# First layer: queries times summed keys and values, head by head on two halves of the TensorE array

## The chip, the cores and the metric

The kernel runs on one core of a Trainium2 chip. A core has five engines with queues of their own: TensorE (PE: products and transposes), VectorE (DVE), ScalarE (ACT), GpSimd (POOL) and SyncE (SP, which here issues DMAs). PE's loading of a stationary operand has a row of its own in the profile, PEld. Matrix results go to PSUM, which has eight banks of 128 partitions x 512 f32. The metric is the device time of one execution in microseconds. Before the change it is 1399.87 us, the median of three runs (1397.45 to 1400.35).

## The reference

Eight sequences x[b] of 512 positions with 512 features go through two attention layers. The first, which the change touches, has eight heads of 64 features and normalises queries and keys apart from each other:

```python
xn = _ln(x, ln_w, ln_b)
q = xn @ Wq + bq
k = xn @ Wk + bk + (1.0 - src_mask) * -1000000.0
q = softmax(q.reshape(b, t, h, dh), axis=-1)      # over a head's 64 features
k = softmax(k.reshape(b, t, h, dh), axis=1)       # over the 512 positions
v = ((xn @ Wv + bv) * src_mask).reshape(b, t, h, dh)
att = einsum('bnhd,bnhl->bhdl', k, v)             # one 64 x 64 matrix per head
y = einsum('bnhd,bhdl->bnhl', q, att).reshape(b, t, d)
hh = _ln(y, ln2_w, ln2_b) * (1.0 + scale) + shift # scale, shift: from the condition
return x + silu(hh) @ W_out + b_out
```

The second layer is attention with 16 heads of 32 features and a softmax over 512 positions. The change leaves it alone.

## The kernel before

**Tiling.** P = 128; a sequence (a block, b = 0 to 7) has four chunks c of 128 positions and its features four groups i of 128, which are two heads each, u = 0 and 1. Weights and activations of the projections are split into a high and a low part (type f32r) and multiplied in three combinations, 12 products of 128x128x512 for each output tile (`project`, L852). The products of this change are plain f32.

**First layer, per block.** `l0_k` (L910) makes the keys' exponentials. `values` (L863) makes the values, `l0_kn` (L928) transposes the keys' exponentials. `l0_att` (L941) sums keys times values over the positions: 32 products of 128x64x64, two heads in two halves of the array's columns. It scales the result into `ab` (buffer `bWk`, one copy): for each feature group i a 128x130 matrix with the two heads' 64x64 blocks on its diagonal, zeros elsewhere, and two columns of ones, one per head. `l0_q` (L967) makes the queries' exponentials. `l0_y` (L982) transposes them (`qT`, buffer `yT`: features on partitions) and multiplies each chunk of `qT` by `ab`. The ones' columns give each head's sum of exponentials, so VectorE takes the reciprocal of these (`rd`) and multiplies (`y`, buffer `xc`). Then come `normalize` (L772), `hidden` (L874) and `output` (L896). The loop over b puts `l0_y` of the block before between the key products of the next: `run(mix(l0_y(b - 1), first, 4, 6))` (L1341) takes four steps of the one, then six of the other, a step ending at each `yield`.

**The order of the work.** Nothing is issued as it is written. Every call is recorded as an operation with an estimated duration (`_takes`: an f32 product takes 1.668 ns per moving column and at least 62). A planner (`Order.pack`, L368) then simulates the engines. Each takes the ready operation with the lowest key, which is the order of writing in the first of 12 rounds and afterwards the latest start by the round before; the round with the shortest planned end is issued, each engine's instructions in the order of planned starts. `order.together(takes)` (L228) makes one operation of several PE calls, with the given duration. Where PE passes between such a group and single calls the planner adds ENTER = 95 or LEAVE = 150 ns (L180, L452). All PSUM tiles of names `mm`, `S`, `ST`, `a` share the eight banks, given out in the order of writing, except that a later tile may take one if two or more are free. In the profile every instruction has L483, the line that issues the recorded calls; operations are told apart by their tiles, and PSUM tiles all read `mm`.

Of the kernel before, what the change touches and what calls it, by code (L numbers as in the profile page):

```python
# [14 lines left out]
F32 = mybir.dt.float32  # L15
F32R = mybir.dt.float32r
AF = mybir.ActivationFunctionType
ALU = mybir.AluOpType
# [3 lines left out]
P = 128  # L22
# [2 lines left out]
EPS = 1e-5  # L25
MASK = 1.0e6
MM = 216
TR = 107

COLS = {"ln_w": 4, "ln_b": 4, "ln2_w": 4, "ln2_b": 4, "b_emb": 8, "mask": 32}  # L30
# [156 lines left out]
class Room:  # L187
# [19 lines left out]
    def next(self):  # L207
        if self.free and self.head in self.queue:
            return self.queue.pop(self.head)
        if self.loose and len(self.free) > 1 and self.queue:  # L210
            return self.queue.pop(min(self.queue, key=lambda i: self.queue[i].key))
# [317 lines left out]
def kernel(ctx: ExitStack, tc: tile.TileContext, x, cond, mask0, mask1, w0, w1, out):  # L529
    real, order = tc.nc, Order(tc)  # L530
    nc = order
# [6 lines left out]
    sm = order.pool(ctx.enter_context(tc.tile_pool(name="sm", bufs=2)), each=2)  # L538
# [7 lines left out]
    def big(tag, name, dtype=F32, shape=(P, 512)):  # L546
        t = sb.tile(list(shape), dtype, name=name, tag=tag, bufs=BUFS[tag])
        if tag == "stk":
            nc.gpsimd.memset(t[:, :, 0:1].bitcast(F32), 0.0)
        return t  # L550

    def bank(tag, name, parts=P):
        tag = {"S": "mm", "ST": "mm", "a": "mm"}.get(tag, tag)
        return ps.tile([parts, 512], F32, name=name, tag=tag, bufs=BANKS[tag])
# [4 lines left out]
    def chunk(i):  # L559
        return slice(i * P, (i + 1) * P)  # L560
# [174 lines left out]
    def prep_emb(l):  # L735
        ssb = []
        for h in range(2):
            ep = mm_bank(f"ep{l}{h}")
            for t in range(2):
                raw = W[l]["we"][2 * h + t]  # L740
                for cg in range(4):
# [3 lines left out]
                    )  # L745
                yield 4 * MM
            ev = big("y", f"ev{l}{h}")
            nc.vector.tensor_copy(ev, ep)
            sp = mm_bank(f"sp{l}{h}")
            for j in range(ND):  # L750
                nc.tensor.matmul(sp[:, 8 * j : 8 * j + 8], ev[:, chunk(j)], sel8, start=True, stop=True)
                yield 2 * MM
            t = const.tile([P, ND, 8], F32, name=f"emb{l}{h}")
# [18 lines left out]
    def normalize(srcs, tag, dve=False):  # L772
        s, n = tag[0], len(srcs)
        mv = sm.tile([P, NC, 2], F32, name=f"mv{tag}", tag="mv" + s)
        for c in range(n):
            st = sm.tile([P, 6], F32, name=f"st{tag}{c}", tag="st" + s)
            nc.vector.bn_stats(st, srcs[c])
            nc.vector.bn_aggr(mv[:, c, :], st)
        ve = sm.tile([P, NC], F32, name=f"ve{tag}", tag="ve" + s)
        nc.gpsimd.tensor_scalar(ve[:, :n], mv[:, :n, 1], 1.0, EPS, ALU.mult, ALU.add)  # L780
        rstd = sm.tile([P, NC], F32, name=f"rs{tag}", tag="rs" + s)
        nc.gpsimd.tensor_tensor(rstd[:, :n], ve[:, :n], mhalf[:, :n], ALU.pow)
        if not dve and "L1" in tag:
            nm = sm.tile([P, NC], F32, name=f"nm{tag}", tag="nm" + s)
            nc.gpsimd.tensor_tensor(nm[:, :n], mv[:, :n, 0], rstd[:, :n], ALU.mult)
            nc.gpsimd.tensor_scalar(nm[:, :n], nm[:, :n], -1.0, 0.0, ALU.mult, ALU.add)
            for c in range(n):
                nc.scalar.activation(srcs[c], srcs[c], AF.Identity, bias=nm[:, c : c + 1], scale=rstd[:, c : c + 1])
            return
        if not dve:  # L790
            nm = sm.tile([P, NC], F32, name=f"nm{tag}", tag="nm" + s)
            nc.gpsimd.tensor_scalar(nm[:, :n], mv[:, :n, 0], -1.0, 0.0, ALU.mult, ALU.add)
        for c in range(n):
            if dve:
                nc.vector.tensor_scalar(
                    srcs[c], srcs[c], mv[:, c, 0:1], rstd[:, c : c + 1], ALU.subtract, ALU.mult
                )
                continue
            nc.gpsimd.tensor_scalar(
                srcs[c], srcs[c], nm[:, c : c + 1], rstd[:, c : c + 1], ALU.add, ALU.mult  # L800
            )
# [34 lines left out]
    def transpose_x(l, b, tag="mm"):  # L836
# [3 lines left out]
        for j in range(ND):  # L840
            tp = bank(tag, f"xp{l}{b}{j}")
            for c in range(NC):
                nc.tensor.transpose(tp[:, chunk(c)], xs[c][:, chunk(j)], ident)
                yield TR
            h, o = alloc(j)
# [6 lines left out]
    def project(pt, left, right, lsl, rsl):  # L852
        n = 3 * ND
        i = 0
        for a, r in ((0, 0), (0, 1), (1, 0)):
            for j in range(ND):
# [3 lines left out]
                i += 1  # L860
                yield MM

# [11 lines left out]
    def hidden(l, b, tag="mm"):  # L874
# [4 lines left out]
        for j in range(ND):  # L879
            tp = bank(tag, f"hp{l}{b}{j}")  # L880
            for c in range(NC):
                nc.tensor.transpose(tp[:, chunk(c)], ys[c][:, chunk(j)], ident)
                yield TR
            h, o = alloc(j)
# [43 lines left out]
    def l0_kn(b):  # L928
        ke = st.pop(("ke", b))
        kn = []  # L930
        for c in range(NC):
            tp = bank("S", f"kt{b}{c}")
            for i in range(4):
                nc.tensor.transpose(tp[:, chunk(i)], ke[i][:, chunk(c)], ident)
                yield TR
            t = big("A", f"kn{b}{c}")
# [4 lines left out]
    def l0_att(b):  # L941
        kn, vs, rk = st.pop(("kn", b)), st.pop(("L0", "v", b)), st.pop(("rk", b))
        at = bank("a", f"at{b}")
        for i in range(4):
            for c in range(NC):
                for u in range(2):
                    h = slice(P * i + 64 * u, P * i + 64 * u + 64)
                    nc.tensor.matmul(
                        at[64 * u : 64 * u + 64, 64 * i : 64 * i + 64],
                        kn[c][:, h],  # L950
                        vs[c][:, h],
                        start=(c == 0),
                        stop=(c == NC - 1),
                    )
        ab = big("bWk", f"ab{b}", shape=(P, 4, 130))
        nc.gpsimd.memset(ab, 0.0)
        nc.gpsimd.memset(ab[0:64, :, 128:129], 1.0)
        nc.gpsimd.memset(ab[64:128, :, 129:130], 1.0)
        at4 = at[:, 0:256].rearrange("p (i e) -> p i e", i=4)
        for u in range(2):  # L960
            r = slice(64 * u, 64 * u + 64)
            nc.vector.tensor_tensor(
                ab[r, :, r], at4[r], rk[r].unsqueeze(2).broadcast_to([64, 4, 64]), ALU.mult
            )
        st["ab", b] = ab

    def l0_q(b):  # L967
# [14 lines left out]
    def l0_y(b):  # L982
        qe, ab = st.pop(("qe", b)), st.pop(("ab", b))
        qt = []
        for i in range(4):
            tp = bank("S", f"qt{b}{i}")
            for c in range(NC):
                nc.tensor.transpose(tp[:, chunk(c)], qe[c][:, chunk(i)], ident)
                yield TR
            t = big("yT", f"qT{b}{i}")  # L990
            nc.scalar.copy(t, tp)
            qt.append(t)
        ys = []
        for c in range(NC):
            y = big("xc", f"yL0{b}{c}")
            for hf in range(2):
                yp = bank("ST", f"yp{b}{c}{hf}")
                for u in range(2):
                    i = 2 * hf + u
                    nc.tensor.matmul(  # L1000
                        yp[:, 130 * u : 130 * u + 130], qt[i][:, chunk(c)], ab[:, i, :], start=True, stop=True
                    )
                    yield MM
                y3 = yp[:, 0:260].rearrange("p (u e) -> p u e", u=2)
                rd = sm.tile([P, 2, 2], F32, name=f"rd{b}{c}{hf}", tag="rd")
                nc.vector.reciprocal(rd, y3[:, :, 128:130])
                nc.vector.tensor_tensor(
                    y[:, 256 * hf : 256 * hf + 256].rearrange("p (u h d) -> p u h d", u=2, h=2),
                    y3[:, :, 0:128].rearrange("p u (h d) -> p u h d", h=2),
                    rd.unsqueeze(3).broadcast_to([P, 2, 2, 64]),  # L1010
                    ALU.mult,
                )
            ys.append(y)
        normalize(ys, f"bL0{b}")
        st["L0", "ys", b] = ys
# [200 lines left out]
    def l1_rden(b, tag="mm", chunks=range(NC)):  # L1216
        dn = st["dn", b]
        dp = bank(tag, f"dp{b}{chunks[0]}")
        for c in chunks:
            nc.tensor.transpose(dp[:, chunk(c)], dn[:, chunk(c)], ident)  # L1220
            yield TR
        rd = sm.tile([P, NC, 4, 4], F32, name=f"rdd{b}{chunks[0]}", tag="rdd")
# [5 lines left out]
    def l1_y(b, tag="mm", chunks=range(NC), dve=False):  # L1228
        rd, yT = st["rd", b], st["yT", b]
        ys = []  # L1230
        for c in chunks:
            tp = bank(tag, f"yt{b}{c}")
            for g in range(4):
                nc.tensor.transpose(tp[:, chunk(g)], yT[g][:, chunk(c)], ident)
                yield TR
            y = big("xc", f"yL1{b}{c}")
# [83 lines left out]
    for b in range(B + 1):  # L1320
# [37 lines left out]
        elif b > 0:  # L1358
            load_x("L0", b + 1, x[b + 1])
        l0_att(b)  # L1360
        if b == 0:
            run(prep_emb("L0"))
# [63 lines left out]
    for _ in range(LEAD):  # L1426
        next(maxes)
    TAIL = 36 * TR + 48 * MM
    HEAD = 72 * MM
    NEXT = 16 * TR + 72 * MM  # L1430
# [49 lines left out]
    b = B - 1  # L1480
# [50 lines left out]
```

## Time and profile before

| | before |
|---|---|
| median of three runs | 1399.87 us |
| profiled execution | 1399.57 us |
| its span, first to last instruction | 1397.8 us |
| granted TensorE clock, mean | 0.993 |
| PE, PEld busy | 1363.6, 949.7 us |
| DVE, ACT, POOL busy | 1057.1, 703.1, 639.0 us |

The page is one profiled execution. A group line gives operation, `output<-inputs`, shape and count, the busy time, the mean duration of one in ns, then the idle time before it and what ended it. PE durations overlap, since the next product starts while the last drains; what one costs is read from start to start in the timeline, whose lines give the start in us, the duration of the merged stretch, engine, operation and count. In PE rows `64*128` means 64 rows and 128 columns of the array; the two numbers after it are partitions and moving columns. The list of a tile's instructions gives the shortest, median and longest duration in ns, and the first and last start. The first layer lasts until about 540 us; the rest is the second layer.

### The profile page before, as it was taken

The page shows a single profiled execution, that of the slowest core. Times are in us where ns is not written, and L with a number is a line of the kernel's source. Part 1 is how long each engine was busy: PE and PEld are TensorE (multiplying, and loading weights), DVE is VectorE, ACT ScalarE, POOL GpSimd, SP SyncE. Part 2 cuts the span into 40 slices and gives each one's busy share as a digit, 9 for nine tenths or more (in the row PEclk, how much of TensorE's full clock was granted, in tenths as well). Part 3 has the DMA queues.
Part 4 walks back from the last instruction along what each step waited for, and adds up shares of the span by engine and source line. Part 5 has one row for each costly group of instructions (what it writes and reads, how often), then busy time and mean ns, then how long its engine had stood idle before and what let it go on. Part 6 is the DMA issues. An engine that isn't in the chain of part 4 may idle for free.

```text
span 1397.8 us, 20898 instructions
## 1 busy us (share of the span) xinstructions
PE 1363.6 (98%) x7419; PEld 949.7 (68%) x7419; DVE 1057.1 (76%) x1815; ACT 703.1 (50%) x1336; POOL 639.0 (46%) x716
## 2 busy tenths in 40 slices
PE   7999999999999999999999999999999999999987
PEld 4788788888888687456566566666666666666645
DVE  7676676666767567987878778778778778878876
ACT  3242323333235252555745755854854764764673
POOL 4213404133232312767437528527636646655663
PEclk9999999999999999999999999999999999999998
DMA  6333203022231366344462563554544545445222
GB/s 223 130 115 105 93 8 99 18 82 90 70 99 34 120 195 166 87 133 110 124 183 64 148 162 92 148 143 104 154 126 123 138 119 145 133 107 155 72 63 69
DMA packets 77365, 158.88 MB, mean 114 GB/s; under 512 B 8550, under 2 KB 8662, under 8 KB 77236
## 3 DMA queue, kind: packets, MB, share of 16 engines
q1 hardware_dynamic: 77144, 157.41, 39.7%
q8 instruction: 59, 0.97, 0.3%
q14 instruction: 46, 0.38, 0.1%
q10 hardware_dynamic: 52, 0.04, 0.0%
q0 software_dynamic: 64, 0.08, 0.0%
HBM read 104.93 MB, written 50.48 MB: 111 GB/s over the span
## 4 chain that ended last, share of the span: by engine, by line
PE 92%; DVE 3%; DMA 2%; ACT 1%; issue 1%; POOL 0%; SPq 0%; DVEq 0%; ACTq 0%; POOLq 0%
PE mm L483 92%; DMA qst<-z 1%; DVE nm L483 1%; DMA qst<-dWq 1%; DVE mi L483 1%; ACT mm L483 0%; ACT y L483 0%; DVE A L483 0%; DVE xc L483 0%; DMA rawL0Wk<-in_L_cond_Wk 0%; DMA dWq<-hl 0%; DVE y L483 0%; ACT z L483 0%; DVE mm L483 0%; DVE Wol L483 0%
## 5 line engine op out<-in xcount | busy, mean ns | idle before, releaser
L483 POOL TENSOR_TENSOR A<-A,A 128x512 f32<-128x512 f32 x231 | 308.1, 1354 | 238.5 <-PE mm L483 173.2
L483 DVE TENSOR_REDUCE nm<-mm 128x1 f32<-128x512 f32 x512 | 332.4, 682 | 73.0 <-PE mm L483 70.2
L483 ACT ACTIVATE A<-mm 128x512 f32<-128x512 f32 x450 | 253.4, 601 | 160.4 <-PE mm L483 157.8
L483 PE MATMUL mm<-kst,qst 98*128 98x512 f32 x512 | 202.9, 421 | 4.1 <-DMA qst<-dWq 2.7
L483 PE MATMUL mm<-qst,kst 106*128 106x512 f32 (+1 forms) x528 | 193.1, 406 | 2.4 <-DMA qst<-z 1.4
L483 PEld LDWEIGHTS mm<-kst,qst 98*128 98x128 f32 x512 | 97.5, 193 | 80.2 <-issue 29.0
L483 PE MATMUL mm<-A,v 128*32 128x512 f32 (+1 forms) x932 | 141.2, 586 | 0.0
L483 PEld LDWEIGHTS mm<-qst,kst 106*128 106x128 f32 x528 | 97.3, 190 | 53.7 <-issue 21.9
L483 POOL TENSOR_TENSOR y<-y,bo 128x512 f32<-128x512 f32 x60 | 78.2, 1309 | 109.9 <-DMA y<-in_x 107.3
L483 PE MATMUL mm<-Wvh,xT 128*128 128x512 f32 x384 | 120.3, 403 | 0.0
L483 PE MATMUL mm<-xT,Wkh 128*128 128x512 f32 x384 | 114.7, 409 | 2.0 <-DVE xT L483 1.7
L483 DVE TENSOR_TENSOR A<-A,A 128x512 f32<-128x512 f32 x91 | 97.8, 1083 | 10.9 <-PE mm L483 10.0
L483 POOL TENSOR_SCALAR v<-bWv,cols 128x512 f32<-128x512 f32 x64 | 47.0, 745 | 122.6 <-PE mm L483 111.2
L483 ACT ACTIVATE y<-mm,shL,scL 128x128 f32<-128x128 f32 (+1 forms) x144 | 76.4, 530 | 49.3 <-PE mm L483 47.1
L483 PE MATMUL mm<-ident,xc 128*128 128x128 f32 x512 | 88.1, 282 | 10.0 <-DVE xc L483 5.3
L483 PEld LDWEIGHTS mm<-ident,xc 128*128 128x128 f32 x512 | 63.6, 143 | 37.9 <-DVE xc L483 8.6
L483 PEld LDWEIGHTS mm<-xT,Wkh 128*128 128x128 f32 x384 | 69.9, 190 | 21.8 <-ACT A L483 4.2
L483 PEld LDWEIGHTS mm<-Wvh,xT 128*128 128x128 f32 x384 | 71.4, 189 | 15.8 <-issue 1.1
L483 ACT ACTIVATE mm<-mm,shL,scL 128x128 f32<-128x128 f32 (+2 forms) x152 | 76.1, 501 | 5.5 <-PE mm L483 5.5
L483 PE MATMUL mm<-xT,Wqh 128*128 128x512 f32 x256 | 76.0, 396 | 0.0
L483 DVE SCALAR_TENSOR_TENSOR v<-mm,cols,v 128x512 f32<-128x512 f32 x64 | 47.8, 746 | 35.4 <-PE mm L483 35.2
L483 ACT ACTIVATE hl<-mm,bcol 128x512 fp32r<-128x512 f32 x64 | 44.1, 689 | 53.6 <-PE mm L483 45.3
(215 smaller groups left out, 2647.2 us busy)
## 6 DMA issues: line engine op xcount, KB each, us to landing
kst<-dWk SPq DMA_DIRECT2D x96, 256.0 KB
qst<-dWq SPq DMA_DIRECT2D x96, 256.0 KB
dWk<-hl SPq DMA_DIRECT2D x32, 512.0 KB
dWq<-hl SPq DMA_DIRECT2D x32, 512.0 KB
xc<-in_x SPq DMA_DIRECT2D x32, 256.0 KB
y<-in_x SPq DMA_DIRECT2D x32, 256.0 KB
x<-y SPq DMA_DIRECT2D x32, 256.0 KB
xc<-x SPq DMA_DIRECT2D x32, 256.0 KB
```

The lines of the kernel that those rows point to most:

```text
L483: getattr(engine, method)(*args, **kw)
```

## The change

`ab` becomes a 128x4x65 tile: for each feature group the two heads' 64x64 matrices stand one above the other, head u on partitions 64u to 64u + 63, with one column of ones beside them. There are no zeros any more; one multiplication on VectorE fills it where two did. In `l0_y` each chunk has eight products, four groups by two heads: 64 rows of `qT` (the head's features) by 65 columns of `ab`. The heads u = 0 lie on the upper half of the array's rows and write one PSUM bank, the heads u = 1 on the lower half and write another. The eight form one group for the planner, with a duration of YP = 640 ns. VectorE has two reciprocals and two multiplications per chunk as before, now by u with all four groups instead of by pairs of groups. There is one `yield` per chunk where there was one per product.

```diff
+YP = 640.0
...
-        ab = big("bWk", f"ab{b}", shape=(P, 4, 130))
-        nc.gpsimd.memset(ab, 0.0)
-        nc.gpsimd.memset(ab[0:64, :, 128:129], 1.0)
-        nc.gpsimd.memset(ab[64:128, :, 129:130], 1.0)
+        ab = big("bWk", f"ab{b}", shape=(P, 4, 65))
+        nc.gpsimd.memset(ab[:, :, 64:65], 1.0)
         at4 = at[:, 0:256].rearrange("p (i e) -> p i e", i=4)
-        for u in range(2):
-            r = slice(64 * u, 64 * u + 64)
-            nc.vector.tensor_tensor(
-                ab[r, :, r], at4[r], rk[r].unsqueeze(2).broadcast_to([64, 4, 64]), ALU.mult
-            )
+        nc.vector.tensor_tensor(ab[:, :, 0:64], at4, rk.unsqueeze(2).broadcast_to([P, 4, 64]), ALU.mult)
...
-            for hf in range(2):
-                yp = bank("ST", f"yp{b}{c}{hf}")
-                for u in range(2):
-                    i = 2 * hf + u
-                    nc.tensor.matmul(
-                        yp[:, 130 * u : 130 * u + 130], qt[i][:, chunk(c)], ab[:, i, :], start=True, stop=True
-                    )
-                    yield MM
-                y3 = yp[:, 0:260].rearrange("p (u e) -> p u e", u=2)
-                rd = sm.tile([P, 2, 2], F32, name=f"rd{b}{c}{hf}", tag="rd")
-                nc.vector.reciprocal(rd, y3[:, :, 128:130])
+            yp = [bank("ST", f"yp{b}{c}{u}") for u in range(2)]
+            with order.together(YP):
+                for i in range(4):
+                    for u in range(2):
+                        r = slice(64 * u, 64 * u + 64)
+                        nc.tensor.matmul(
+                            yp[u][:, 65 * i : 65 * i + 65], qt[i][r, chunk(c)], ab[r, i, :], start=True, stop=True
+                        )
+            yield 4 * MM
+            for u in range(2):
+                y3 = yp[u][:, 0:260].rearrange("p (i e) -> p i e", i=4)
+                rd = sm.tile([P, 4], F32, name=f"rd{b}{c}{u}", tag="rd")
+                nc.vector.reciprocal(rd, y3[:, :, 64])
                 nc.vector.tensor_tensor(
-                    y[:, 256 * hf : 256 * hf + 256].rearrange("p (u h d) -> p u h d", u=2, h=2),
-                    y3[:, :, 0:128].rearrange("p u (h d) -> p u h d", h=2),
-                    rd.unsqueeze(3).broadcast_to([P, 2, 2, 64]),
+                    y.rearrange("p (i u d) -> p u i d", i=4, u=2)[:, u],
+                    y3[:, :, 0:64],
+                    rd.unsqueeze(2).broadcast_to([P, 4, 64]),
                     ALU.mult,
                 )
```

## The prediction

> **What bounds the kernel now.** I read the page first, then the chain of waits, the stretches of the first layer, and the instructions of the tile that the change rewrites.
>
> ```profile
> PE 1363.6 (98%) x7419; PEld 949.7 (68%) x7419; DVE 1057.1 (76%) x1815; ACT 703.1 (50%) x1336; POOL 639.0 (46%) x716
> ...
> PE 92%; DVE 3%; DMA 2%; ACT 1%; issue 1%; POOL 0%; SPq 0%; DVEq 0%; ACTq 0%; POOLq 0%
> ...
> 180.00:240.00 60.00, 60.00 (x367) 49.88 (x366) 40.76 (x87) 19.30 (x36) 17.47 (x27) 1.00 0.18 58
> 240.00:300.00 60.00, 60.00 (x366) 50.01 (x365) 40.07 (x80) 20.69 (x38) 17.68 (x29) 1.00 0.17 58
> ```
>
> TensorE (PE) carries 92% of the chain that ended last. The last two lines are 60 us stretches of the first layer (PE, weight loads, DVE, ACT, POOL, granted clock, DMA share): PE has work in all 60 us at full clock, DVE is busy 40 of 60. So in this layer a microsecond put on or taken off PE's queue is a microsecond of the kernel, and VectorE has a third of its time spare. There is no PE wait in those stretches that a shorter dependency could give back.
>
> The products to be replaced, among the wide products of the next block's keys:
>
> ```profile
> L483 PEld LDWEIGHTS mm<-bWk,yT x256: 187/191/193, 77.0 to 504.5; 128*128 128x128 f32 x128
> L483 PE MATMUL mm<-bWk,yT x256: 272/275/278, 77.2 to 504.6; 128*128 128x130 f32 x128
> ...
> 77.24 1.06 PE L483 MATMUL mm<-bWk,yT 128*128 128x130 f32 x8
> 78.05 1.17 PE L483 MATMUL mm<-xhL,Wkh 128*128 128x512 f32 x4
> 79.06 0.63 PE L483 MATMUL mm<-xlL,Wkh 128*128 128x512 f32 x2
> 79.53 1.06 PE L483 MATMUL mm<-bWk,yT 128*128 128x130 f32 x8
> ```
>
> 128 products are 256 instructions: each f32 product runs as two, each with a weight load of its own. From one chunk's products to the next is 79.53 - 77.24 = 2.29 us. Six 512-column instructions lie in it; four in a row take 0.93 us where nothing else is between (86.38 to 87.31 in the same timeline), so 0.233 each, 1.40 in all. That leaves **0.89 us for eight instructions, 0.112 each**: 32 chunks x 0.89 = 28.6 us. This is all that the change can touch on PE.
>
> **Is 0.112 us the moving columns or the weight load?** Both fit: 130 columns in the two passes of an instruction (a 512-column f32 instruction of the wide heads' groups steps 0.43 us, so 130 columns need 0.108), and a load of 128 columns. After the change only the first halves, to 65 columns. A product with 8 moving columns tells them apart:
>
> ```profile
> 174.66 0.97 PEld L483 LDWEIGHTS mm<-sel,y 128*128 128x128 f32 x8 [0.88 <-DVE y L483]
> ...
> 112.33 1.95 PEld L483 LDWEIGHTS mm<-v,A 128*64 128x64 f32 x64 [0.37 <-issue]
> ```
>
> Here eight loads of 128 columns span 0.97 us, the last of them 0.19: (0.97 - 0.19) / 7 = **0.111 us per load**, though only 8 columns move. So the load alone sets that pace. In the second line (keys times values, today already in two column halves) 64 loads of 64 columns take 1.95 us, 0.029 each. At the rate above 64 columns need 0.055; so two halves' loads run side by side there.
>
> **The new group on PE.** Per chunk it has eight products of 64 rows, 128 stationary columns and 65 moving ones: 16 instructions, 16 loads, where there were 8 and 8. The number of stationary columns is not halved. By the Trainium skill (TensorE: Matmul & The Clock Gate, section LDWEIGHTS) a load's time goes with its columns, not its rows. No ordinary 64-row load stands in this trace; loads of 106 and 98 rows have the mean of those with 128 (190 to 193 ns). Bounds for 16 instructions:
> - moving data alone, two halves at once: 8 x 0.054 = 0.43, with 0.007 between the two of a pair (the step inside a pair of the column halves) 0.48 us;
> - loads, two halves at once as the column halves do it: 8 x (0.112 + 0.007) = 0.95 us;
> - loads one after the other: 16 x 0.112 = 1.79 us.
>
> I take **0.95**: the row nearest to it is that of the 8-column products, a load-bound stream, and side-by-side loading is what the column halves show. Against today's 0.89 the product itself then gains nothing; it loses 0.06 per chunk, 4 x 0.06 = 0.23 us per block.
>
> The skill has a rule that says otherwise: the same page, Packing small matmuls, gives a pack the span of one product plus 4 ns for each further tile, which here is the 0.43 to 0.48 us bound (an estimate by that page). By the rule a block's products fall from 3.58 to 1.92 us. Its measured cases there are 512 columns wide, where the load hides; here 65 columns move per 128 loaded, so I go with the row.
>
> **Going in and out of the split array.** Today's products have the same 128x128 form as their neighbours. The new ones don't. TensorEngine Tiling (Array Packing), Key Properties, says that a change of tiling mode drains the array, without a price. The trace has one for 64 rows, a short transpose of the biases:
>
> ```profile
> 478.48 0.40 PE L483 MATMUL mm<-Wqh,xlL 128*128 128x512 f32 x1
> 478.81 0.46 PE L483 MATMUL mm<-ident,y 64*128 64x64 f32 x4
> 479.20 0.97 PE L483 MATMUL mm<-Wqh,xlL 128*128 128x512 f32 x3
> 480.00 0.39 PE L483 MATMUL mm<-Wqh,xhL 128*128 128x512 f32 x1
> ```
>
> From 478.48 to 480.00 is 1.52 us. Four wide instructions cost 0.93 and four transposes at their inner step of 0.062 cost 0.25, so **0.34 us** goes into entering and leaving. The groups of four heads in the second layer agree: 689.58 to 691.95 is 2.37, less five wide (1.16) and two steps of 0.434 (0.87), 0.34 again. It is paid once for each unbroken run of groups. Following the order of work as written, the four groups of a block now follow each other (four steps of this generator, then six of the keys). What can break the run is banks: a group takes two at once of eight, and gives them back after a reciprocal and a multiplication for each:
>
> ```profile
> L483 DVE TENSOR_TENSOR xc<-mm,rd 128x256 f32<-128x256 f32 x64 | 27.1, 424 | 2.2
> ...
> L483 DVE RECIPROCAL rd<-mm 128x4 f32<-128x4 f32 x64 | 11.1, 173 | 6.1 <-PE mm L483 5.1 <-ACT Wkh L483 0.4
> ```
>
> That is 2 x (0.17 + 0.42) = 1.2 us of VectorE per group against 0.64 in the plan for PE. One or two banks are held by the keys, so two or three groups go at once and the rest wait for VectorE, with wide products put between: two to three runs per block, 2.5 in the middle, one and four at the ends. 2.5 x 0.34 = 0.85 us.
>
> **The rest of the change.** VectorE's 64 reciprocals and 64 multiplications keep their count and size; I cost their new strides at nothing, covered by its spare third. For the block matrix, 16 multiplications of 64x256 (422 ns) become 8 of 128x256 (424 ns), 3.4 us less on DVE; eight large clearings (up to 0.53 us) and 16 small ones on POOL become eight small ones. Nobody waits for either: the first block matrix is written at 55.8 us and first read at 77.2. Without that cover it would be worth some 0.4 us per block. The one clearing that stays still waits at the head of POOL's queue for the single buffer, as now. No DMA is added or moved. A group needs all four transposed queries where a product needed one: the last copy to SBUF takes 0.59 us and six wide products (1.40 us) stand before the first group, so that wait is hidden; everything on PE would stand behind it. The planner gets 640 ns for a group; if it lasts 0.95, VectorE starts each pair 0.3 us later than planned, which its idle third absorbs.
>
> **Sum.** Per block 4 x 0.95 + 0.85 - 4 x 0.89 = 1.08 us; eight blocks, **+8.6 us**. The profiled execution (1399.57 us around a span of 1397.8) goes to 1408.2; it lies 0.3 under the median, so the runs go from 1399.87 to **1408.5 us**. With one to four runs of groups per block it is 1403 to 1413.
>
> **Rivals.**
> - *Half-height loads are quicker, or both halves' loads hide: faster.* At 0.48 us a group, 4 x 0.48 + 0.85 - 3.58 = -0.81 per block, 1393.4 us. For it: the packing rule. Against it: loads that keep their duration with fewer rows. Break-even is at (3.58 - 0.85) / 4 = 0.68 us per group; below it this decides.
> - *The plan's own figure, 0.64, is true:* -0.17 per block, 1398.5 us, not to be told from no change. No row supports it, but other constants of the planner (216 for a wide product, 107 for a transpose) stand close to the trace.
> - *The two halves' loads take turns:* 1.79 us a group, 4 x 0.90 + 0.85 = 4.5 per block, 1435 us. Against it: the column halves load together; but two row halves are seen nowhere here.
> - *Two banks at once starve PE:* groups break into four runs and PE waits some 0.5 us per block for VectorE: 0.23 + 4 x 0.34 + 0.5 = 2.1 per block, 1416.6 us. Against it: PE finds wide products to do in all 60 us of a stretch.
>
> **How the numbers follow.** My forecast 57%, the fast loads 13%, the plan's figure 12%, loads in turn 10%, starved banks 8%. The measurement tells about 0.2% (2.8 us) from no change. Faster holds the fast loads, 0.13; same holds the plan's figure and the edge of my own range, 0.14; slower the rest, 0.73. The range 1395 to 1421 holds my forecast, the plan's figure, the starved banks and the weaker half of the fast loads; it leaves out loads in turn and the full fast case, under 2 in 10. My forecast alone is 1403 to 1413.
>
> **What the new profile would show.** 512 product instructions of 64x65 with 512 loads of 64x128; a whole group of 16 stepping 0.95 us, pairs 0.12 apart; gaps of a third of a microsecond around two or three runs per block; VectorE's rows unchanged at 173 and 424 ns; the second layer as long as before. Pairs 0.06 apart would overthrow the load bound, single loads 0.11 apart the side-by-side loading. A group standing alone every time, or a second layer that changes by more than 2 us because the planner settles elsewhere, would make the size wrong.

## The result and the profile after

| | before | after |
|---|---|---|
| median | 1398.66 us (1396.94 to 1400.35) | 1410.68 us (1410.42 to 1412.03) |
| profiled execution | 1399.57 us | 1410.69 us |
| its span | 1397.8 us | 1408.9 us |

The median of before is that of the runs made beside those of the changed kernel. The ratio is 1.0088 (95% interval 1.0071 to 1.0105): the change makes the kernel 12.0 us slower. The page of the kernel after, its busy times and the engines' shares of the chain that ended last:

```profile
PE 1376.7 (98%) x7675; PEld 948.1 (67%) x7675; DVE 1054.7 (75%) x1806; ACT 704.3 (50%) x1336; POOL 634.7 (45%) x701
...
PE 92%; DVE 4%; DMA 2%; ACT 2%; issue 1%; POOL 0%; ACTq 0%; DVEq 0%; SPq 0%
```

TensorE (PE) carries the end as before and has 13 us more to do, with 256 more instructions. The two stretches of the first layer, columns as before (PE, weight loads, DVE, ACT, POOL, granted clock, DMA share):

```profile
180.00:240.00 60.00, 59.47 (x346) 46.71 (x345) 41.54 (x96) 19.39 (x36) 11.00 (x19) 1.00 0.14 48
240.00:300.00 60.00, 59.50 (x388) 48.07 (x387) 38.27 (x75) 19.50 (x36) 17.41 (x29) 1.00 0.18 60
```

PE, busy in all 60 us before, now misses half a microsecond in each. In these stretches VectorE and the clock are about where they were. The products that took the place of the old ones, in the list of the tile `bWk` (shortest, median and longest duration in ns, first and last start):

```profile
L484 PEld LDWEIGHTS mm<-bWk,yT x512: 182/188/188, 80.8 to 521.9; 64*128 64x128 f32 x171
L484 PE MATMUL mm<-bWk,yT x512: 272/272/321, 80.8 to 522.0; 64*128 64x65 f32 x171
```

The first two groups of them in PE's timeline:

```profile
79.77 1.07 PE L484 MATMUL mm<-xhL,Wkl 128*128 128x512 f32 x4
80.77 1.11 PE L484 MATMUL mm<-bWk,yT 64*128 64x65 f32 x16
81.80 1.19 PE L484 MATMUL mm<-xhL,Wkh 128*128 128x512 f32 x4
82.84 0.62 PE L484 MATMUL mm<-xlL,Wkh 128*128 128x512 f32 x2
83.39 1.11 PE L484 MATMUL mm<-bWk,yT 64*128 64x65 f32 x16
84.43 0.73 PE L484 MATMUL mm<-xlL,Wkh 128*128 128x512 f32 x2
```

There are 512 product instructions of 64x65 (256 products) with 512 loads of 64x128. A weight load of 64 rows lasts 188 ns where one of 128 rows lasted 191. Every one of the 32 groups stands alone between wide products. In the single records of a group, the two halves of a pair start 7 ns apart and the next pair starts 105 ns later; only the first step is longer (154). So **a pair of half-height instructions takes 0.112 us, as long as one full-height instruction took before**, and there are as many pairs as there were instructions. What is new is the way in and out: from 80.77 to 81.80, and a start later than 0.233 us behind the product ahead of it. In the records, from the start of the last wide product ahead to that of the second one behind is 1.694 us (0.319, 1.039, 0.335) against 1.363 before (0.235, 0.811, 0.317): 0.33 us for each group.

Something else moved as well. PE's timeline some 20 us later in the same block:

```profile
103.91 3.09 PE L484 MATMUL mm<-Woh,hhL 128*128 128x512 f32 x11 [0.51 <-ACT hhL L484]
106.92 0.34 PE L484 MATMUL mm<-v,A 128*64 128x64 f32 x4
...
115.60 1.97 PE L484 MATMUL mm<-v,A 128*64 128x64 f32 x60
```

PE waits for `hhL`, the input of the output projection, and the 64 instructions that sum keys times values are issued in two pieces, at 106.92 and 115.60 us. Neither was so before.

**Where the time lies.** I give every PE instruction of three whole blocks (from the first product of the fourth block to that of the seventh) the time until the next one starts, a wait going to the instruction ahead of it, and divide by three. The second table follows the end of the first layer: how much later than before the first and the 65th `mm<-kst,qst` of the second layer start, and how much longer the span is, each in one profiled execution; 48 output products of the first layer still follow the first `kst,qst`. The other kernels of both tables are the experiments below.

| us per block | before | after | e1 | e9 | e5 | e6 | e8 | e11 |
|---|---|---|---|---|---|---|---|---|
| the products | 3.25 | 4.16 | 3.25 | 4.16 | 4.16 | 2.51 | 3.11 | 2.35 |
| projections of queries, keys, values | 34.72 | 35.20 | 34.92 | 35.35 | 35.02 | 35.04 | 34.57 | 34.77 |
| transposes, with the wait for `hhL` | 5.65 | 6.44 | 6.43 | 6.43 | 5.66 | 5.65 | 5.65 | 5.65 |
| output projection | 11.61 | 11.71 | 11.91 | 11.92 | 11.40 | 11.40 | 11.40 | 11.40 |
| sums of keys times values | 2.02 | 2.16 | 2.16 | 2.16 | 2.02 | 2.02 | 2.02 | 2.02 |
| block | 57.24 | 59.67 | 58.67 | 60.02 | 58.25 | 56.62 | 56.74 | 56.19 |

| us against before | after | e1 | e9 | e5 | e6 | e7 | e8 | e11 |
|---|---|---|---|---|---|---|---|---|
| first `kst,qst` | +17.9 | +9.6 | +19.9 | +9.0 | -5.0 | +0.2 | -4.1 | -6.4 |
| 65th `kst,qst` | +9.9 | +1.7 | +13.4 | +5.3 | -6.2 | -6.9 | -10.8 | -14.9 |
| span | +11.1 | +3.4 | +15.5 | +3.5 | -7.0 | -6.8 | -10.2 | -14.0 |

So the first layer is 17.9 us longer, not 8.6, and some 8 us of it are given back where the second layer begins. PE's waits in that transition (us in all, times, longest), before (500 to 620 us) and after (500 to 640), show the larger part of it:

```profile
PE mm L483 <- DVE mi L483: 3.2, 2, 2.7
PE mm L483 <- DVE xT L483: 1.7, 1, 1.7
PE mm L483 <- issue: 1.3, 1, 1.3
```

```profile
PE mm L484 <- DVE nm L484: 0.7, 1, 0.7
PE mm L484 <- DMA qst<-z: 0.6, 1, 0.6
PE mm L484 <- DVE mi L484: 0.2, 1, 0.2
```

Before, PE stood still there for some 6 us, for VectorE and for nothing that the profile shows. In the planned order of the kernel after, these waits are gone. The rest fits the clock. Stretches of the transition before, then after (columns as above; the clock is the third number from the end):

```profile
552.00:558.00 6.00, 6.00 (x15) 4.66 (x16) 3.27 (x5) 0.97 (x2) 0.00 (x0) 0.50 0.97 225
572.00:576.00 4.00, 3.69 (x12) 2.86 (x13) 3.85 (x7) 1.51 (x3) 0.00 (x0) 0.58 0.11 15
```

```profile
540.00:600.00 60.00, 58.60 (x281) 39.92 (x279) 54.08 (x86) 27.94 (x51) 26.29 (x25) 1.00 0.59 166
```

Before, the granted clock falls to 0.50 and 0.58 behind PE's waits, and the wide products step 0.427 us there instead of 0.233: about 3 us for the fifteen that run from 552 to 558. After the change it is 1.00. This part varies between executions: among those of the kernel before that ran beside the experiments, the ones with a mean granted clock of 0.995 or 0.996 took 1395.8 to 1397.6 us, the ones with 0.989 to 0.991 took 1400.2 to 1403.1.

### The profile page after: what moved, and what is told of

It is laid out like the page before. It is cut to its first block, busy times and chain, and to the rows that moved or that the text cites. A ratio compares the mean times of both kernels' runs of the same rounds, so it can differ in the third digit from the quotient of the medians.

```text
span 1408.9 us, 21374 instructions
## 1 busy us (share of the span) xinstructions
PE 1376.7 (98%) x7675; PEld 948.1 (67%) x7675; DVE 1054.7 (75%) x1806; ACT 704.3 (50%) x1336; POOL 634.7 (45%) x701
## 4 chain that ended last, share of the span: by engine, by line
PE 92%; DVE 4%; DMA 2%; ACT 2%; issue 1%; POOL 0%; ACTq 0%; DVEq 0%; SPq 0%
PE mm L484 92%; DVE nm L484 2%; DMA qst<-z 1%; DVE A L484 1%; ACT y L484 1%; DVE y L484 0%; DVE xc L484 0%; ACT mm L484 0%; DMA out<-y 0%; DVE mi L484 0%; DMA rawL0Wk<-in_L_cond_Wk 0%; POOL xc L484 0%; ACT hhL L484 0%; DMA xc<-in_x 0%; ACT z L484 0%
## 5 line engine op out<-in xcount | busy, mean ns | idle before, releaser
L484 PE MATMUL mm<-ident,xc 128*128 128x128 f32 x512 | 91.2, 283 | 10.8 <-DVE xc L484 5.7
L484 ACT ACTIVATE A<-mm,km 128x512 f32<-128x512 f32 x32 | 22.1, 692 | 106.5 <-DVE km L484 84.9
```

Of the source, the lines that this page charges most:

```text
L484: getattr(engine, method)(*args, **kw)
```

## The experiments

Each kernel is one edit away from the kernel after unless its heading says otherwise.

**e1: the order and banks of the change, with the products of before.** One group per chunk, two banks, duration 640 ns, but four products of 128 rows by 130 columns on the whole array. The edit is shown against the kernel before.

```diff
+            yp = [bank("ST", f"yp{b}{c}{u}") for u in range(2)]
+            with order.together(YP):
+                for i in range(4):
+                    nc.tensor.matmul(
+                        yp[i // 2][:, 130 * (i % 2) : 130 * (i % 2) + 130], qt[i][:, chunk(c)], ab[:, i, :],
+                        start=True, stop=True,
+                    )
+            yield 4 * MM
             for hf in range(2):
-                yp = bank("ST", f"yp{b}{c}{hf}")
-                for u in range(2):
...
-                    yield MM
```

> The changed kernel with its groups, its two banks at a time and its order of work kept, but each group holds the four 128x128 products of 130 columns of the kernel before. Theory A (the loss is the passing into and out of the split array, 0.33 us for each of 32 groups that stand alone): 1410.7 - 10.6 = 1400 us, within 2 us. Rival B (the loss is the new order of work: groups of two banks delay the rest of the block): it stays at 1408 us or above.

1404.16 us (1402.41 to 1405.55), ratio 1.0040 (1.0027 to 1.0053): between the two. The grouping alone costs about 6 us, half of the change's loss, and it does so without any splitting of the array. PE's waits name the same stop as in the kernel after, there too 3.0 us in six waits:

```profile
PE mm L484 <- ACT hhL L484: 3.0, 6, 0.5
```

In the table e1 has the two pieces of the sums and the wait for `hhL` as well: 1.43 us per block more than before, 0.5 of it the wait, the rest in more passages between transposes, sums and wide products. Its PE instructions stand in the order of the kernel after, tile by tile, the products apart. So the loss has two causes of similar size, and what remains for the split array is what e1 lacks.

**e2: two chunks in one group.** 16 products, four banks, 16 groups instead of 32. It halves the passages.

```diff
-        for c in range(NC):
-            yp = [bank("ST", f"yp{b}{c}{u}") for u in range(2)]
-            with order.together(YP):
+        for c2 in range(0, NC, 2):
+            yps = [[bank("ST", f"yp{b}{c2 + k}{u}") for u in range(2)] for k in range(2)]
+            with order.together(2 * YP):                   # the products of chunks c2 and c2 + 1
```

> The changed kernel with two chunks (16 products, four banks) in one group, so 16 groups instead of 32. Theory A: 16 passings of 0.33 us fewer, 1410.7 - 5.3 = 1405.4 us. If the order of work around the groups also costs something (the plan's own end is 10 us earlier here), down to 1400 us. If passings cost nothing and only the loads do, no change, 1410.7 us.

1414.04 us (1412.32 to 1416.03), ratio 1.0110 (1.0095 to 1.0125): a miss, slower than the change. A block (taken as in the table) is 58.4 us long, 1.25 less than after the change, as expected. The last block undoes it. Its groups in PE's timeline:

```profile
530.51 2.00 PE L484 MATMUL mm<-bWk,yT 64*128 64x65 f32 x32
...
535.18 2.00 PE L484 MATMUL mm<-bWk,yT 64*128 64x65 f32 x32
```

After the change the four groups of that block stand at 513.7 to 521.1. With four of the eight banks asked for at once the planner starts them 17 us later, and by the 65th `kst,qst` the kernel is 1.7 us behind the one after the change. That it is the banks which hold them there was not tried apart.

**e3: 128 columns moving instead of 65.** The further columns are ones; they are written to PSUM and not used.

```diff
-        ab = big("bWk", f"ab{b}", shape=(P, 4, 65))
-        nc.gpsimd.memset(ab[:, :, 64:65], 1.0)
+        ab = big("bWk", f"ab{b}", shape=(P, 4, 128))
+        nc.gpsimd.memset(ab[:, :, 64:128], 1.0)
...
-                            yp[u][:, 65 * i : 65 * i + 65], qt[i][r, chunk(c)], ab[r, i, :], start=True, stop=True
+                            yp[u][:, 128 * i : 128 * i + 128], qt[i][r, chunk(c)], ab[r, i, :], start=True, stop=True
```

> The changed kernel with 128 moving columns per product instead of 65 (the added ones carry ones and are not used). Theory A (the weight load of 128 columns sets the pace of a pair, 0.112 us): no change, 1410.7 us within 1.5 us, and pairs still step 0.112 us. Rival C (moving columns set the pace): a pair takes some 0.05 us more, 8 x 32 pairs, +13 us, 1424 us.

1411.95 us (1411.1 to 1413.15), 1.3 us more than after the change. The list of the tile:

```profile
L484 PEld LDWEIGHTS mm<-bWk,yT x512: 182/188/188, 80.1 to 522.8; 64*128 64x128 f32 x171
L484 PE MATMUL mm<-bWk,yT x512: 272/272/373, 80.1 to 522.9; 64*128 64x128 f32 x171
```

With twice the moving columns the median instruction and the step of a pair (7 and 105 ns) are the same; only the first step of a group grows from 154 to 206 ns, 32 x 0.052 = 1.7 us. So from 65 to 128 the moving columns do not set the pace.

**e4: quarters of the array.** The other side of the same question: each product in two of 64 stationary columns, four products on four quarters, as many moved columns per quarter.

```diff
+                    for w in range(2):
                         for u in range(2):
                             r = slice(64 * u, 64 * u + 64)
+                            n = slice(64 * w, 64 * w + 64)
-                            nc.tensor.matmul(yp[u][:, 65 * i : 65 * i + 65], qt[i][r, chunk(c)], ab[r, i, :], ...)
+                            nc.tensor.matmul(yp[u][n, 65 * i : 65 * i + 65],
+                                             qt[i][r, P * c + 64 * w : P * c + 64 * w + 64], ab[r, i, :], ...)
```

YP is 500 ns here.

> The changed kernel with each product cut again into two halves of 64 stationary columns, so that four products lie on four quarters of the array; twice the instructions, half the columns per load. Theory A (a load goes by its columns, loads of different parts run side by side): four products step 0.06 to 0.08 us instead of two in 0.112, a group falls from 0.90 to about 0.55 us, 32 x -0.35 = -11 us, about 1400 us. Rival D (a load has a fixed price, or the loads of more parts take turns): a group lasts 1.7 us or more, 1436 us.

1399.0 us (1397.69 to 1400.4), ratio 1.0005 (0.9997 to 1.0014): all of the loss is gone, with twice the instructions. The products do not do this alone: in the profiled execution the first `kst,qst` still comes 5.5 us later than before (PE's waits for `hhL` are 6.3 us here), and the transition takes 6.1 us off. The list of the tile:

```profile
L484 PEld LDWEIGHTS mm<-bWk,yT x1024: 129/134/137, 79.6 to 510.1; 64*64 64x64 f32 x171
L484 PE MATMUL mm<-bWk,yT x1024: 216/218/268, 79.7 to 510.1; 64*64 64x65 f32 x171
```

A group in PE's timeline:

```profile
79.65 0.70 PE L484 MATMUL mm<-bWk,yT 64*64 64x65 f32 x32
80.28 1.21 PE L484 MATMUL mm<-xhL,Wkh 128*128 128x512 f32 x4
```

Four instructions start 7 ns apart and the next four some 0.06 us after the first: half the columns to load, half the step. From the group to the product behind it is 0.63 us instead of 1.04. With e3 this shows that **the stationary columns to load set the pace**, and that four parts of the array load side by side.

**e5: the products of the change in the order of before.** The planner sees four calls per chunk, one bank each time, of 217 ns, as before the change. The first three are placeholders that issue nothing; the fourth issues all eight products. `many` is what makes the planner add its passage times, and is off for these groups. PE's order in the first layer comes out as before, but for a few instructions near its end.

```diff
+                if k < 3:
+                    order.add("tensor", [("skip", (yp[-1], qt[k][:, chunk(c)], ab[:, k, :]), {})], 130 * 1.668, 200.0)
+                else:
+                    with order.together(130 * 1.668):      # the eight products
...
+                yield MM
...
-                many = len(o.calls) > 1
+                many = len(o.calls) > 1 and takes > 300.0
```

> The eight half-array products of the changed kernel, issued together, but planned as the four products of the kernel before: same durations, same requests for one bank at a time, same steps, so PE's order is that of the kernel before. Theory A+B (two costs: 0.33 us per passing, 32 passings, and on top of it the changed order): without the changed order, 1398.0 + 10.6 = 1408.6 us. If the changed order were all of the loss and the passing were hidden: 1398 us.

1403.74 us (1403.1 to 1407.33), ratio 1.0038 (1.0025 to 1.0052): the order of before removes 7 of the 12 us, and the time lies 5 us under what was expected. PE's timeline:

```profile
77.81 1.11 PE L485 MATMUL mm<-bWk,yT 64*128 64x65 f32 x16
78.85 1.19 PE L485 MATMUL mm<-xhL,Wkh 128*128 128x512 f32 x4
79.87 0.61 PE L485 MATMUL mm<-xlL,Wkh 128*128 128x512 f32 x2
80.42 1.11 PE L485 MATMUL mm<-bWk,yT 64*128 64x65 f32 x16
```

From group to group is 2.61 us with the same six wide products in which before stepped 2.29: 0.32 for the split array, now by itself. There is no wait for `hhL` and no divided sum. In the first layer this gives +9.0 us, near the prediction's 8.6, though some 1.7 us of shorter output products (0.21 per block, see e9) are taken off in it; the transition then gives 5.5 back.

**e6: e5 with the quarters of e4.**

> As the run with half-array products in the order of the kernel before, but with quarters of the array (64 stationary columns). A group measured 1.29 us from the product before it to the one after next, against 1.36 us for the four whole-array products: 32 x -0.076 = -2.4 us, 1395.6 us. If the gain by shorter loads shows only where PE waits anyway: 1398 us or more.

1391.8 us (1390.4 to 1395.69), ratio 0.9953 (0.9938 to 0.9968). Against e5 the products take 1.65 us less per block (4.16 to 2.51); eight blocks are 13.2, and the times differ by 11.9. It went 4 us lower than expected; the shorter steps of the output products (0.21 us per block, 1.7 in eight) are part of that, and e9 tells where they come from.

**e7: the kernel before, with one step per chunk.** Its four products per chunk are planned one by one and ask for one bank each time, but a step of the generator is a whole chunk, as in the change.

```diff
                     nc.tensor.matmul(
                         yp[:, 130 * u : 130 * u + 130], qt[i][:, chunk(c)], ab[:, i, :], start=True, stop=True
                     )
-                    yield MM
...
+            yield 4 * MM
```

> The kernel before with one step per chunk in place of four and nothing else: whole-array products, each asking for one bank. The plan then puts the 16 products of a block one after another. If one step per chunk is what spoils the order in the changed kernel, it is slower by the 6 us that the wide products in groups cost, 1404 us; if it is the group's asking for two banks at once, it stays at 1395 to 1398 us (the plan's own end is 2.7 us earlier).

1393.5 us (1390.42 to 1394.93), ratio 0.9960 (0.9945 to 0.9974): faster than before. All four chunks' products now follow each other:

```profile
76.80 0.40 PE L483 MATMUL mm<-xhL,Wkl 128*128 128x512 f32 x1
77.04 3.75 PE L483 MATMUL mm<-bWk,yT 128*128 128x130 f32 x32
```

In the first layer nothing is gained (+0.2 at its end, a block of 57.2 us). So the larger step alone does not spoil the order as in e1. What is left is that a group is one operation, with two banks, the planner's passage times and 640 ns where four calls have 867; these were not tried apart. The whole gain of e7 lies in the transition, where its waits are as short as those after the change. No cause in the products was found for that: the planner's rounds settled on another order there.

**e8: e6 with one step per chunk.**

> Quarters of the array in the order of the run with one step per chunk: the four groups of a block follow each other, so the array is split once per block. Theory A: per block 0.32 + 0.63 + 3 x 0.50 + 0.34 - 0.47 = 2.3 us in place of 4 x 0.90 = 3.6, eight blocks -10 us: 1386 to 1389 us. If VectorE, which needs 1.2 us per group to empty its banks, holds PE up: 1395 us or more.

1388.35 us (1387.73 to 1389.44), ratio 0.9925 (0.9913 to 0.9938), as expected. The groups stand in twos, but PE then waits inside the second two:

```profile
197.87 1.17 PE L485 MATMUL mm<-bWk,yT 64*64 64x65 f32 x64
198.97 0.50 PE L485 MATMUL mm<-xhL,Wkh 128*128 128x512 f32 x1
199.40 0.33 PE L485 MATMUL mm<-bWk,yT 64*64 64x65 f32 x2
200.33 1.16 PE L485 MATMUL mm<-bWk,yT 64*64 64x65 f32 x62 [0.60 <-ACT A L485]
```

The plan of 4 x 217 ns for a chunk is far from the 0.63 us that it takes; whether the third group comes too early for that reason is what e11 asks. The profile names ScalarE's `A` as the end of the wait; whether a bank or data came with it was not taken apart.

**e9: the kernel after with the buffer of before.** The instructions are those of the change; the buffer `bWk` is 520 columns wide again (4 x 130), instead of the 512 that its other tiles need, so what is laid out behind it lies 32 bytes further on in each partition.

```diff
-        ab = big("bWk", f"ab{b}", shape=(P, 4, 65))
+        ab = big("bWk", f"ab{b}", shape=(P, 520))[:, 0:260].rearrange("p (i e) -> p i e", i=4)
```

> The changed kernel, instruction for instruction, with the block matrix's buffer 520 columns wide as in the kernel before, of which it uses 260; what is placed behind it in SBUF moves back to the places of the kernel before. In the runs so far, wide products of the output step 0.228 us in kernels with the narrower buffer and 0.233 us in those with 520 columns. Theory E (placement sets that step): it returns to 0.233 us, some 0.33 us per block, +3 us, 1413.5 us. If the split array itself makes the following wide products quicker: no change, 1410.7 us and 0.228.

1414.35 us (1413.29 to 1415.13), ratio 1.0101 (1.0083 to 1.0119), 3.7 us above the change, 1.8 by the two ratios, whose intervals overlap; so the trace has to say whether it is this. PE's instructions stand in the same order in both. Wide products of the output projection, after the change and in e9:

```profile
297.71 1.07 PE L484 MATMUL mm<-Wol,hhL 128*128 128x512 f32 x4
298.62 1.07 PE L484 MATMUL mm<-Woh,hlL 128*128 128x512 f32 x4
```

```profile
296.30 1.10 PE L484 MATMUL mm<-Wol,hhL 128*128 128x512 f32 x4
297.23 1.10 PE L484 MATMUL mm<-Woh,hlL 128*128 128x512 f32 x4
```

Four take 0.91 us in the one and 0.93 in the other. Over the first layer the mean step is 0.227 to 0.228 us in all kernels whose buffer has 512 columns (after, e2 to e6, e8, e11) and 0.233 in those with 520 (before, e1, e7, e9). A block is 60.02 us in e9 and 59.67 after the change.

**e10: the kernel before with 544 columns.** The heads' matrices are 136 apart, so the buffers behind lie 128 bytes further on than with 512.

```diff
-        ab = big("bWk", f"ab{b}", shape=(P, 4, 130))
+        ab = big("bWk", f"ab{b}", shape=(P, 4, 136))
...
-                        yp[:, 130 * u : 130 * u + 130], qt[i][:, chunk(c)], ab[:, i, :], start=True, stop=True
+                        yp[:, 130 * u : 130 * u + 130], qt[i][:, chunk(c)], ab[:, i, 0:130], start=True, stop=True
```

> The kernel before, instruction for instruction, with the block matrix's buffer 544 columns wide (a multiple of 128 bytes, as 512 is) instead of 520. Theory E: wide products of the output step 0.228 us, -3 us, 1395.5 us. Otherwise no change, 1398.5 us and 0.233.

1399.68 us (1396.15 to 1405.75), ratio 1.0008 (0.9992 to 1.0024): no difference that can be told. The output products keep stepping 0.232 to 0.233 us, and a block 57.2. So a shift by a multiple of 128 bytes does not bring the shorter step either. By which rule the place of a buffer sets it stays open.

**e11: e8 planned at its true length.** Four calls of 140 ns, 0.56 us per chunk.

```diff
-                    order.add("tensor", [("skip", (yp[-1], qt[k][:, chunk(c)], ab[:, k, :]), {})], 130 * 1.668, 200.0)
+                    order.add("tensor", [("skip", (yp[-1], qt[k][:, chunk(c)], ab[:, k, :]), {})], 140.0, 200.0)
...
-                    with order.together(130 * 1.668):
+                    with order.together(140.0):
```

> The run with quarters of the array and one step per chunk, where the planner gives a chunk's products 0.56 us, about what they last, instead of 0.87. If a truer duration helps the plan: a few us below 1388 us. If the settled plan is as much chance as cause: 1386 to 1395 us.

1385.4 us (1384.88 to 1385.61), ratio 0.9895 (0.9875 to 0.9914): the fastest of all, 14 us under the kernel before and 25 under the change. The pause of e8 is gone; the third and fourth groups of a block now have wide products ahead of them:

```profile
196.42 1.17 PE L485 MATMUL mm<-bWk,yT 64*64 64x65 f32 x64
197.52 0.73 PE L485 MATMUL mm<-xhL,Wkh 128*128 128x512 f32 x2
198.18 0.70 PE L485 MATMUL mm<-bWk,yT 64*64 64x65 f32 x32
198.81 0.73 PE L485 MATMUL mm<-xhL,Wkh 128*128 128x512 f32 x2
```

Of its 14.0 us of span, 6.4 are gained in the first layer and the rest in the transition. It is one settled plan against another: how much of the 3 us against e8 is the truer duration, and how much the chance of the plan, is not shown.

## Why the prediction was right, and which of its terms were not

The forecast was 1408.5 us (1403 to 1413), and 1410.68 was measured. Sign and mechanism of the main term hold, and its size within a fifth; three terms that it did not have nearly cancel.

- **The bound.** Right: in the first layer PE is the bound on both sides of the change, and what is put on its queue lengthens the layer.
- **"The load alone sets that pace."** Right, and shown from both sides: twice the moving columns change nothing in the step (e3), half the stationary columns halve it (e4). The rule of the Trainium skill (TensorE: Matmul & The Clock Gate, Packing small matmuls), from which the prediction estimated 0.43 to 0.48 us for a chunk, doesn't give the time here, where a pair steps 0.112 us and its 65 moving columns alone would need 0.054 (an estimate from the 0.43 us of 512 columns).
- **0.95 us for a group.** Somewhat too high. The 7 ns inside a pair do not come on top of the load; the pair steps 0.112, not 0.119, so a chunk's products are 8 x 0.112 = 0.90, what they were. The term of +0.23 per block is about zero.
- **0.34 us for a passage.** Right: 0.33. The **2.5 runs of groups per block** were the mis-sized term: all four groups stand alone, which the prediction had as its upper end (its lower end, one run, is 1404 us by the same sum, not 1403). 4 x 0.335 = 1.34 per block for 0.23 + 0.85 = 1.08. The clean measure is e9 against e1, which have the same order and buffer and differ in the products: 1.35 us per block, 10.3 at the end of the first layer; 8.6 was forecast.
- **VectorE, POOL and the block matrix at nothing.** Right in the rows of the kernel after:

```profile
L484 DVE TENSOR_TENSOR xc<-mm,rd 128x256 f32<-128x256 f32 x64 | 27.2, 425 | 2.2
...
L484 DVE RECIPROCAL rd<-mm 128x4 f32<-128x4 f32 x64 | 11.3, 177 | 14.2 <-PE mm L484 14.1
...
L484 DVE TENSOR_TENSOR bWk<-mm,rk 128x256 f32<-128x256 f32 x8 | 3.4, 422 | 19.1 <-PE mm L484 19.1
```

- **"That wait is hidden", and the order of work at nothing.** This step failed. PE doesn't stand still ahead of a group, but the first group of a block comes at 80.77 us where the first product came at 77.24, and behind it the output's inputs are late and the sums are cut in two: 1.43 us per block, +9.6 us at the end of the first layer (e1). Starved banks, the rival, had a loss of this kind and size in mind (0.5 us of waiting per block), but put it at VectorE; the wait that the profile shows is 0.5 us per block for ScalarE's `hhL`. Why the planner orders so was followed in its rules only: a group needs two banks free in one moment, and calls that are ready earlier take them one by one. e7 shows that the step's length alone isn't it; the banks, the passage times and the planned 640 ns were not separated, so the cause within the planner stays open.
- **The second layer "as long as before".** Wrong by more than the 2 us that the prediction had named as a warning: from the first `kst,qst` to the end it is 6.8 us shorter. The waits of before in the transition are gone, as they are in e1 and e7, whose products are those of before, and after the change and in e1 the fall of the clock behind them is gone too. So it belongs to the planned order and not to the split array. Its size is less sure: e1 and e9, in the same order, are 6.2 and 4.3 us shorter there (in e9 the granted clock is 0.76 from 590 to 597 us).
- **The place of the buffers**, not thought of: about -0.35 us per block, from `bWk` shrinking from 520 to 512 columns (e9).

At the end of the first layer the sum is order +9.6, split array +10.3, place -2.0: +17.9. The transition and the second layer take 6.8 off, which leaves the 11.1 us of the span. That the total came within 2.2 us of the forecast is in part luck: its own mechanism was worth 10, and the three others came to about +1.

## What to carry to other kernels

These f32 products, with 65 to 128 moving columns for 128 stationary ones, are bound by the load of their stationary columns: splitting the rows of the array saves nothing, splitting its columns does. Count a price for every unbroken run of split products (0.33 us here) and count the runs in the worst order that the planner may choose. When a change alters how an order is planned (one operation for four, two banks for one), measure the new order with the old arithmetic first, and the new arithmetic in the old order: here each cost about as much in the first layer, and a plan with nearly the true length of the same work came out 3 us faster. The waits of the transition cost more than their own length, since the clock fell behind them: look at the granted clock of single stretches, not only at its mean.

## What the runs showed that was not expected

- The step of a wide output product depends on where buffers lie: 0.227 to 0.228 us with a `bWk` of 512 columns, 0.232 to 0.233 with 520 or 544, with the mean granted clock between 0.993 and 0.995 in the kernels compared; the kernel after and e9 differ in nothing else.
- Four quarters of the array load and multiply at once, 7 ns apart: four products of 64x64 by 65 per 0.06 us, against 0.112 for two products of 64x128 by 65. The same work goes at half the step with twice the instructions; a whole group takes 0.63 us instead of 1.04.
